# Deformable layer: turning tiles on TensorE by ordinary products with the identity instead of the transpose mode

## The chip, the cores and the metric

The kernel runs on one core of a Trainium2 chip. The metric is the device time of one execution, in microseconds (us). TensorE (PE) multiplies matrices into PSUM, VectorE (DVE) and ScalarE (ACT) work element by element, GpSimd (POOL) issues the indirect DMAs (gathers) here, and SyncE (SP) issues the ordinary DMAs.

## The reference

Four layers are applied one after the other to x of shape (8, 96, 64, 64) in float32: a selective scan over pixels, a layer in the frequency domain, a selective scan in four directions with sampled positions, and a deformable convolution. Each takes the normalised output of the one before. Only the last one is touched by the change. Cut to its core, for each of eight images of 96 channels and 64 x 64 pixels:

```python
om     = conv3x3(x, [offset_w, mask_w]) + [offset_b, mask_b]   # 18 offsets and 9 masks a pixel
mask   = sigmoid(om[18:27])
py, px = pixel position + tap position + offset                # 9 positions a pixel
s[k]   = bilinear(x, py[k], px[k]) * mask[k]                   # 9 sampled vectors of 96 channels
out    = sum over k of weight[:, :, k] @ s[k] + bias
```

The kernel also adds the layer's input to its output.

## The kernel before

Four functions write the four layers one after the other; `layer3` is the deformable one. The pixels of an image stand in 32 tiles of 128, and eight images make 256 tiles. A plan written by hand (`Plan`) gives every piece of work a slot; in each slot the pieces are issued in the fixed order first, pool, main, turn, pe, act, dve, late, sp. Each engine then runs its own pieces strictly in that order and waits on semaphores where data come from another engine. One slot holds one tile, so slot P + i belongs to tile i of the image that starts at slot P.

**What one tile takes.** `gather` (line 1889) has POOL issue nine indirect DMAs, one for each tap, that bring the four neighbours of 128 pixels into the tile `v` (128 x 9 x 4 x 96, a ring of five buffers). `sums` has DVE multiply `v` with the bilinear weights (line 1908) and add the four neighbours (line 1917) into `s` (128 pixels x 9 x 96, a ring of four buffers). `turn` (line 1929) has PE turn the nine 128 x 96 slices of `s` into 96 x 128, three to a PSUM bank `ps_t` (a ring of three). `keep` (line 1938) has ACT copy the three banks into `smp`. After four tiles `out` (line 1961) multiplies `smp` of 512 pixels with the nine weight matrices into `ps_o`, adds the layer's input by a product with the identity (line 1965), ACT adds the bias (line 1970) and SP stores.

**What one image takes ahead of its tiles.** Eight chunks of 512 pixels are loaded and normalised; `turn(c)` (line 1690) turns a chunk in four pieces into `ps_u`, and ACT copies them to `xt`, from which SP writes the table that the gathers read. `offsets(c)` runs the nine taps of the offset convolution (line 1724, `ps_a`), ACT evicts them (line 1736), `back` (line 1741) turns the 27 x 512 result in four pieces, and ACT copies it to `of` (line 1750). Some thirty small DVE and ACT operations make positions and weights of it. This preparation of an image is put into the slots of the image before it.

So three places turn data: line 1690 four times a chunk, line 1741 four times a chunk, and line 1929 nine times a tile: 256, 256 and 2304 turns. Before the change all three call `nc.tensor.transpose(out, x, identity)`. It loads `x` as the stationary operand and streams the identity through it.

Each buffer ring ties two engines: POOL can be five tiles ahead of DVE (`v`), DVE four tiles ahead of PE (`s`), and PE three banks, which is one tile, ahead of ACT (`ps_t`).

Of the kernel before, what the change touches and what calls it, by code (L numbers as in the profile page):

```python
# [170 lines left out]
class Shared:  # L171
# [21 lines left out]
    def stats_tile(self, layer):  # L193

        return new(self.pool, [CH, NB, 2], f"stats{layer}")

    def rsqrt(self, out, var, pool, tag):

        n = var.shape[1]
        ve = new(pool, [CH, n], f"{tag}_ve")  # L200
        self.nc.vector.tensor_scalar(ve, var, EPS, None, ALU.add)
        self.nc.gpsimd.tensor_tensor(  # L202
            out, ve, self.mhalf[:CH, :].to_broadcast([CH, n]), ALU.pow
        )
# [1417 lines left out]
def layer3(S, src, table, dst, st_in, images):  # L1622
# [3 lines left out]
    tc, nc = S.tc, S.nc  # L1626
    NT = NP // 128
    with ExitStack() as ctx:
# [30 lines left out]
        def image(b, P, n):  # L1659
# [5 lines left out]
            start = P - (60, 27, 42, 46, 50)[min(n, 4)]  # L1665
# [20 lines left out]
            def turn(c):  # L1686
                def pe():
                    im["ps"] = ps = new(psu, [128, NW], "ps_u")
                    for j in range(4):
                        nc.tensor.transpose(  # L1690
                            ps[:, j * CH : (j + 1) * CH],
                            im["x", c][:, j * 128 : (j + 1) * 128],
                            S.ident[:CH, :CH],
                        )

                def act():
                    if c == 0:
                        im["xt"] = new(mp, [128, NT, CH], "xt")
                    nc.scalar.copy(
                        im["xt"][:, 4 * c : 4 * c + 4, :].rearrange("p t c -> p (t c)"),  # L1700
                        im["ps"][:, : 4 * CH],
                    )

                plan.at(start + (6 + c if n != 1 else 2 + c), "pe", pe)
                plan.at(start + (7 + c if n != 1 else 3 + c), "first", act)
# [11 lines left out]
            def offsets(c):  # L1717
                def taps(k0, k1):
                    def run():
                        if k0 == 0:  # L1720
                            im["pa"] = new(psa, [128, NW], "ps_a")
                        for k in range(k0, k1):
                            dy, dx = k // 3, k % 3
                            nc.tensor.matmul(  # L1724
                                im["pa"][: 3 * KT, :],
                                om[:, k, :],
                                xpad[:, 8 * c + dy : 8 * c + dy + 8, dx : dx + IW],
                                start=k == 0,
                                stop=k == KT - 1,
                            )  # L1730

                    return run

                def evict():
                    im["oc"] = new(wp, [3 * KT, NW], "oc")
                    nc.scalar.activation(im["oc"], im["pa"][: 3 * KT, :], AF.Identity, bias=omb)  # L1736

                def back():
                    im["ps"] = ps = new(psu, [128, NW], "ps_u")
                    for j in range(4):  # L1740
                        nc.tensor.transpose(  # L1741
                            ps[:, j * 27 : (j + 1) * 27],
                            im["oc"][:, j * 128 : (j + 1) * 128],
                            S.ident[: 3 * KT, : 3 * KT],
                        )

                def keep():
                    if c == 0:
                        im["of"] = new(mp, [128, NT, 3 * KT], "of")
                    nc.scalar.copy(  # L1750
                        im["of"][:, 4 * c : 4 * c + 4, :].rearrange("p t k -> p (t k)"),
                        im["ps"][:, : 4 * 27],
                    )

                t, two = start + 14 + 2 * c, 1
                if n == 0 and c > 1:
                    t, two = P + c - 2, 0
                elif n == 1:
                    t, two = start + 9 + 3 * c // 2, 0
                plan.at(t, "pe", taps(0, 5))  # L1760
                plan.at(t + two, "pe", taps(5, KT))
                plan.at(t + two + 1, "first", evict)
                plan.at(t + two + 1, "pe", back)
                plan.at(t + two + 2, "first", keep)

# [112 lines left out]
        def tiles(im, b, P, n):  # L1878
# [4 lines left out]
            def tile(i):  # L1883
                t, st, g, j = P + i, {}, i // 4, i % 4

                def gather():
                    st["v"] = new(vp, [128, KT, 4, CH], "v")
                    for k in range(KT):
                        nc.gpsimd.indirect_dma_start(  # L1889
                            out=st["v"][:, k].rearrange("p q c -> p (q c)"),  # L1890
                            out_offset=None,
                            in_=flat,
                            in_offset=bass.IndirectOffsetOnAxis(
                                ap=im["idx"][:, i, k : k + 1], axis=0
                            ),
                        )

                def weights():
                    im["ps_w", g] = new(psw, [128, NW], "ps_w")
                    nc.scalar.copy(  # L1900
                        im["ps_w", g][:, : 4 * KT * 4],
                        im["wt"][:, i : i + 4].rearrange("p t k q -> p (t k q)"),
                    )

                def sums():

                    v3 = st["v"].rearrange("p k q c -> p (k q) c")
                    nc.vector.tensor_tensor(  # L1908
                        v3,
                        v3,  # L1910
                        im["ps_w", g][:, j * 4 * KT : (j + 1) * 4 * KT]
                        .unsqueeze(2)
                        .to_broadcast([128, 4 * KT, CH]),
                        ALU.mult,
                    )
                    st["s"] = new(vp, [128, KT, CH], "s", bufs=4)
                    nc.vector.tensor_reduce(  # L1917
                        st["s"],
                        st["v"].rearrange("p k q c -> p k c q"),
                        mybir.AxisListType.X,  # L1920
                        ALU.add,
                    )

                def turn():
                    st["ps"] = []
                    for k0 in range(0, KT, 3):
                        ps = new(pst, [128, NW], "ps_t")
                        for k in range(3):
                            nc.tensor.transpose(  # L1929
                                ps[:CH, k * 128 : (k + 1) * 128], st["s"][:, k0 + k, :], S.ident  # L1930
                            )
                        st["ps"].append(ps)

                def keep():
                    if j == 0:
                        im["smp", g] = new(wp, [CH, KT, NW], "smp")
                    for k0, ps in zip(range(0, KT, 3), st["ps"]):
                        nc.scalar.copy(  # L1938
                            im["smp", g][:, k0 : k0 + 3, j * 128 : (j + 1) * 128],
                            ps[:CH, :384].rearrange("p (k n) -> p k n", k=3),  # L1940
                        )

                plan.at(t - 1, "pool", gather)
                if j == 0:
                    soon = (n, g) in ((0, 0), (0, 2), (1, 0))
                    plan.at(t - (1 if soon else 3), "act", weights)
                plan.at(t, "main", sums)
                plan.at(t + 1, "turn", turn)
                plan.at(t + 2, "first", keep)

# [91 lines left out]
```

## Time and profile before

| | |
|---|---|
| three executions | 18651.31, 18676.62 (median), 18689.72 us |
| the profiled execution | 18651.78 us, its span 18650.0 us |
| deformable layer, about 14900 to 18650 us | 3750 us |
| there: PE busy | 1813.60 us, 5369 matmul and 5368 weight-load records |
| there: DVE busy | 2641.08 us |
| there: POOL busy | 2224.16 us |
| there: ACT busy | 606.34 us |
| granted TensorE clock there (before it) | 0.68 (0.96) |

An engine's rows come from its own instruction records. PE is shown as two tracks: PEld for the weight loads and PE for the matmuls that follow them. A float32 product that isn't in the transpose mode leaves two records on each track for one call in the program. "Idle before" names what ended the idle time ahead of an instruction: an instruction of another engine, "remote" where no recorded instruction fits the semaphore, or "issue" where the engine waited for no semaphore that the profile shows.

### The profile page before, as it was taken

How to read it: one execution, taken by the hardware profiler on the slowest of the kernel's cores; microseconds unless marked ns; L12 is line 12 of the kernel's file. 1: busy time of each engine (PE TensorE's matmuls, PEld its weight loads, DVE VectorE, ACT ScalarE, POOL GpSimd, SP SyncE). 2: the span in 40 equal slices, each digit the busy share in tenths (PEclk: the TensorE clock that was granted, in tenths of full speed). 3: DMA queues.
4: the chain of work that ended last, by engine and by line, in shares of the span. 5: the costliest groups of instructions: out<-in, count | busy, mean ns of one | idle time of the engine just before them, and what ended most of it. 6: DMA issues, size and time to landing. Idle time of an engine off the chain costs nothing. (4 is left out here: it accounts for less than half of the span.)

```text
span 18650.0 us, 134925 instructions
## 1 busy us (share of the span) xinstructions
PE 14905.1 (80%) x35468; PEld 5346.1 (29%) x35468; DVE 16325.1 (88%) x9561; ACT 10781.0 (58%) x17415; POOL 15401.6 (83%) x9600
## 2 busy tenths in 40 slices
PE   8998998848988898989888889888988855454443
PEld 2222223622323232323233233222332212121111
DVE  7999998549999999999999999999999956677777
ACT  7777876536666666666666666666666611111111
POOL 7999997019999999999999999999999955666665
PEclk8999998869999999999999999999999977666666
DMA  7888887349999999999999999999999944444444
GB/s 121 143 147 140 145 144 121 58 106 152 154 154 153 154 154 152 154 153 153 154 152 155 153 153 153 154 151 155 153 153 154 153 131 136 144 146 144 144 145 128
DMA packets 936948, 2689.54 MB, mean 144 GB/s; under 512 B 273906, under 2 KB 275647, under 8 KB 933389
## 3 DMA queue, kind: packets, MB, share of 16 engines
q1 hardware_dynamic: 788717, 2227.78, 70.6%
q0 software_dynamic: 147456, 453.13, 8.2%
q8 instruction: 279, 4.57, 0.1%
q14 instruction: 496, 4.06, 0.1%
HBM read 579.52 MB, written 87.69 MB: 36 GB/s over the span
## 5 line engine op out<-in xcount | busy, mean ns | idle before, releaser
L345 POOL TENSOR_TENSOR dbu<-dd,brep 128x1024 f32<-128x1024 f32 x3840 | 9027.6, 2359 | 459.6 <-DMA dd<-delta 335.8
L362 PE MATMUL ps_y<-dbu,k_red 128*96 128x512 f32 x15360 | 7526.7, 618 | 732.1 <-DVE dbu L354 714.8
L324 ACT ACTIVATE ps_d<-dd,l_alog 128x512 f32<-128x512 f32 x7680 | 5297.8, 690 | 3479.2 <-DVE dbu L354 3305.7
L1449 DVE TENSOR_TENSOR_SCAN ps_d<-ps_d,dbu 128x1024 f32<-128x1024 f32 x2880 | 6589.1, 2288 | 149.4 <-ACT ps_d L324 120.1
L354 DVE TENSOR_TENSOR dbu<-ps_d,crep 128x1024 f32<-128x1024 f32 x3520 | 4312.0, 1225 | 333.9 <-DVE ps_d L1449 7.3
L362 PEld LDWEIGHTS ps_y<-dbu,k_red 128*96 128x96 f32 x15360 | 2358.0, 166 | 5556.3 <-issue 2885.8
L1889 POOL DMA_INDIRECT v<-t,idx x2304 | 2190.2, 951 | 1431.1 <-issue 695.6
L1917 DVE TENSOR_REDUCE s<-v 128x864 f32<-128x3456 f32 x256 | 1559.3, 6091 | 873.7 <-remote 700.2
L1929 PE MATMUL ps_t<-k_ident,s 128*96 128x128 f32 x2304 | 448.9, 343 | 1272.2 <-issue 872.1
L657 DVE TENSOR_TENSOR_SCAN ps_d<-ps_d,carry,dbu 128x1024 f32<-128x1024 f32 x560 | 1315.1, 2348 | 95.1 <-ACT ps_d L673 82.3
L1938 ACT COPY smp<-ps_t 96x384 f32<-96x384 f32 x768 | 332.2, 474 | 1801.0 <-remote 1112.4
L1428 PE MATMUL ps_a<-xs,rep_w 96*128 96x512 f32 x2048 | 1110.1, 623 | 34.1 <-ACT brep L1436 30.2
L1164 PE MATMUL ps_k<-pad,woff 96*96 96x512 f32 x2304 | 1093.4, 597 | 34.1 <-ACT pad L1141 20.8
L1908 DVE TENSOR_TENSOR v<-v,ps_w 128x3456 f32<-128x3456 f32 x256 | 957.7, 3741 | 46.3 <-ACT smp L1938 29.5
L350 POOL TENSOR_TENSOR dbu<-h,crep 128x1024 f32<-128x1024 f32 x320 | 753.6, 2355 | 126.5 <-DVE h L1449 93.1
L1724 PE MATMUL ps_a<-xpad,l_om 96*27 96x512 f32 x1152 | 654.1, 708 | 164.5 <-issue 164.4
L1929 PEld LDWEIGHTS ps_t<-k_ident,s 128*96 128x96 f32 x2304 | 316.9, 156 | 1470.5 <-issue 1083.3
L1961 PE MATMUL ps_o<-smp,l_w 96*96 96x512 f32 x1152 | 555.6, 637 | 31.4 <-issue 31.3
L202 POOL TENSOR_TENSOR sc<-bn_ve,mhalf 96x1 f32<-96x1 f32 (+1 forms) x2 | 1.2, 621 | 695.9 <-DVE mv L972 695.8
L1164 PEld LDWEIGHTS ps_k<-pad,woff 96*96 96x96 f32 x2304 | 372.0, 164 | 674.0 <-issue 587.0
L1428 PEld LDWEIGHTS ps_a<-xs,rep_w 96*128 96x128 f32 x2048 | 346.4, 190 | 750.1 <-ACT brep L1436 311.5
L1386 POOL TENSOR_TENSOR sp_m<-sp_m,sp_s 128x512 f32<-128x512 f32 x384 | 488.2, 1272 | 30.3 <-ACT sp_s L1374 30.3
(259 smaller groups left out, 17100.6 us busy)
## 6 DMA issues: line engine op xcount, KB each, us to landing
dd<-delta SPq DMA_DIRECT2D x3840, 512.0 KB
v<-t,idx POOLq DMA_INDIRECT x2304
xo<-x SPq DMA_DIRECT2D x128, 192.0 KB
x<-xo SPq DMA_DIRECT2D x128, 192.0 KB
x<-x SPq DMA_DIRECT2D x16, 1536.0 KB
yr<-y SPq DMA_DIRECT2D x12, 1536.0 KB
xn<-x SPq DMA_DIRECT2D x64, 192.0 KB
xh<-x SPq DMA_DIRECT2D x16, 768.0 KB
```

The costliest lines, as they stand in the source:

```text
L324: nc.scalar.activation(g.da[:, i, :], g.dd[:, 0, :], AF.Exp, scale=g.a[:, i : i + 1])
L345: nc.gpsimd.tensor_tensor(g.dbu, g.dd[:, 1:2, :].to_broadcast([128, 2, NW]), g.b(), ALU.mult)
L354: nc.vector.tensor_tensor(g.dbu, g.h, g.c(), ALU.mult)
L362: self.S.nc.tensor.matmul(y, self.red[:, 80 - GC * g.n : 176 - GC * g.n], g.dbu[:, i, :], start=first and i == 0, stop=last and i == 1,)
L657: nc.vector.tensor_tensor_scan(out, da, dbu, carry[:, n : n + 1] if c else 0.0, ALU.mult, ALU.add)
L1164: nc.tensor.matmul(ch["pk"][:HD, :], woff[:, k, m * HD : (m + 1) * HD], pad[:, dy : dy + 8, dx : dx + IW], start=k == 0, stop=k == KT - 1,)
L1428: nc.tensor.matmul(dr["pa"], rep_w[:, k, what, s, :], xs[:CH, k % 2, :], start=True, stop=True,)
L1449: nc.vector.tensor_tensor_scan(out[:, way], da[:, way], dbu[:, way], 0.0, ALU.mult, ALU.add)
L1889: nc.gpsimd.indirect_dma_start(out=st["v"][:, k].rearrange("p q c -> p (q c)"), out_offset=None, in_=flat, in_offset=bass.IndirectOffsetOn ...
L1908: nc.vector.tensor_tensor(v3, v3, im["ps_w", g][:, j * 4 * KT : (j + 1) * 4 * KT] .unsqueeze(2) .to_broadcast([128, 4 * KT, CH]), ALU.mult,)
L1917: nc.vector.tensor_reduce(st["s"], st["v"].rearrange("p k q c -> p k c q"), mybir.AxisListType.X, ALU.add,)
L1929: nc.tensor.transpose(ps[:CH, k * 128 : (k + 1) * 128], st["s"][:, k0 + k, :], S.ident)
```

## The change

All three places call a new helper. It issues an ordinary product with the same operands, `x` as the stationary operand and the identity as the moving one, so the result is the same turned tile. Tiles, buffers, order and everything that reads the result stay as they were.

```diff
+    def turn(self, out, x, ident):
+
+        self.nc.tensor.matmul(out, x, ident, start=True, stop=True)
...
-                        nc.tensor.transpose(
+                        S.turn(
                             ps[:, j * CH : (j + 1) * CH],
                             im["x", c][:, j * 128 : (j + 1) * 128],
                             S.ident[:CH, :CH],
...
-                        nc.tensor.transpose(
+                        S.turn(
                             ps[:, j * 27 : (j + 1) * 27],
                             im["oc"][:, j * 128 : (j + 1) * 128],
                             S.ident[: 3 * KT, : 3 * KT],
...
-                            nc.tensor.transpose(
+                            S.turn(
                                 ps[:CH, k * 128 : (k + 1) * 128], st["s"][:, k0 + k, :], S.ident
                             )
```

## The prediction

> **What bounds the kernel now.** The change touches only the last layer, so I first read the busy times by stretch. From 15023 us, the first gather, to 18600 us, just behind the last, POOL's 2304 gathers are busy for 2190.16 of 3577 us, DVE for 2549.15, PE for 1698.43. No engine is full.
>
> Next I read who waited for whom in that stretch. In each row stand the time in total, how often, and the longest.
>
> ```profile
> DVE s L1917 <- remote: 697.7, 45, 48.5
> POOL v L1889 <- DVE s L1917: 543.5, 51, 22.7
> ```
>
> A gather takes 0.95 us plus an issue gap of 0.30, so 1.25; nine make 11.25 us a tile, and 256 tiles 2880 us of the 3577. The remaining 697 are pauses. POOL pauses because its five `v` buffers are full (51 times, 10.7 us each), and they are full because DVE stood still 45 times for 15.5 us ahead of a sum. DVE alone needs 3.74 + 6.09 = 9.83 us a tile, less than POOL.
>
> Why DVE stands still I read in the timeline of one such place (start, duration, engine, line, operation, idle time before it).
>
> ```profile
> 17057.52 1.45 PE L1961 MATMUL ps_o<-smp,l_w 96*96 96x512 f32 x3
> ...
> 17068.64 1.01 PE L1961 MATMUL ps_o<-smp,l_w 96*96 96x512 f32 x1 [1.79 <-issue]
> ...
> 17081.40 0.95 POOL L1889 DMA_INDIRECT v<-t,idx  x1 [0.30 <-issue]
> ...
> 17086.13 5.28 PE L1724 MATMUL ps_a<-xpad,l_om 96*27 96x512 f32 x6 [0.39 <-issue]
> ...
> 17087.60 0.47 ACT L1938 COPY smp<-ps_t 96x384 f32<-96x384 f32 x1 [26.98 <-remote]
> ...
> 17088.33 6.13 DVE L1917 TENSOR_REDUCE s<-v 128x864 f32<-128x3456 f32 x1 [17.66 <-remote]
> ...
> 17094.72 0.94 POOL L1889 DMA_INDIRECT v<-t,idx  x1 [12.38 <-DVE s L1917]
> ```
>
> The reader should see four steps. From 17058 PE issues one record only every 0.7 or 1.4 us, with "issue" before it; ACT and DVE hear nothing from PE. POOL gathers on until its buffers are full at 17082. Some 4 us later PE is quick again, ACT and DVE start within 2 us, and POOL goes on once DVE has freed a `v`. The profile doesn't name what holds PE up.
>
> It does show what the hold-up counts. I took eight uninterrupted runs of gathers, each from the first gather behind a pause to the last before the next, and read the busy times by stretch. Four runs lie where PE has little besides turns, four where it also prepares the next image.
>
> ```profile
> core 0: us, PE busy (x) PEld busy (x) DVE busy (x) ACT busy (x) POOL busy (x), PEclk, DMA share, GB/s
> 16843.20:16921.60 78.40, 25.65 (x82) 10.30 (x80) 60.79 (x13) 6.16 (x15) 59.50 (x63) 0.67 0.68 202
> 17164.70:17243.20 78.50, 30.79 (x90) 14.81 (x88) 67.35 (x27) 14.98 (x31) 59.61 (x63) 0.65 0.56 167
> 18209.40:18299.10 89.70, 28.63 (x84) 12.84 (x82) 71.45 (x15) 6.37 (x15) 68.04 (x72) 0.63 0.54 159
> 18424.70:18514.30 89.60, 27.31 (x84) 12.84 (x82) 71.36 (x15) 6.26 (x14) 67.98 (x72) 0.63 0.54 159
> 16982.30:17027.00 44.70, 32.55 (x85) 9.84 (x83) 32.66 (x7) 4.39 (x11) 34.01 (x36) 0.77 0.52 153
> 17037.60:17082.30 44.70, 29.77 (x77) 9.40 (x75) 32.76 (x7) 3.68 (x9) 34.01 (x36) 0.73 0.52 154
> 17426.20:17470.90 44.70, 30.21 (x82) 9.48 (x81) 32.72 (x7) 4.13 (x10) 34.01 (x36) 0.77 0.52 153
> 17873.00:17929.00 56.00, 29.04 (x90) 10.45 (x88) 41.05 (x9) 4.75 (x12) 42.55 (x45) 0.74 0.52 154
> ```
>
> The runs last from 44.7 to 89.7 us and hold 36 to 72 gathers, four to eight tiles. But PE's records, matmuls and loads together, number 152 to 178 in each. A run of gathers ends when PE has issued about 165 records, however long that took. Time, gathers and ACT's records (9 to 31) vary too much to be what is counted. So the number of PE records sets how often the layer pauses: 10,134 records in the stretch over 51 pauses are 199 a pause.
>
> [...]
>
> **The change part by part.** Only PE's stream changes; waits, signals, buffers, DMAs and the order stay.
>
> ```profile
> L1961 PE MATMUL ps_o<-smp,l_w 96*96 96x512 f32 x1152 | 555.6, 637 | 31.4 <-issue 31.3
> L1929 PE MATMUL ps_t<-k_ident,s 128*96 128x128 f32 x2304 | 448.9, 343 | 1272.2 <-issue 872.1 <-ACT smp L1938 354.6 <-DVE s L1917 31.6
> ```
>
> *Records.* Line 1961 is called 576 times (64 groups by nine) and has 1152 matmul records, two a call; line 1929 is called 2304 times and has 2304, one a call. So a turn grows from one load and one matmul to two of each: 2 x 2816 = 5632 more records, of which I count 5500 in the stretch (the first image's preparation precedes the gathers). 10,134 become 15,630.
>
> *PE's time.* In the timeline at 17042 us and full clock the turns follow each other every 0.109 us. The nearest ordinary products, 96 columns moving (line 867), come 40 in 3.20 us, 0.080 each, so 128 columns take 0.107, twice for one call: 0.21 in place of 0.11. That is 0.98 us a tile and some 300 us in all, or 600 at half clock. PE has 1879 idle us in the stretch; it is hidden there. If it weren't, 0.98 us of a tile's turn would stand in the chain of a pause.
>
> [...]
>
> *Pauses.* At 199 records a pause, 15,630 make 78.5, 27.5 more. At 10.7 us each that is +294. But a pause lets PE run freely, and after it there are twice the turn records ready; I give each pause 20 more records (half of one tile's 36), so 219: 71.4 pauses, 20.4 more, +218. I take the middle, +256, and a third of the 0.98 us for 75 pauses, +25, since a pause's chain holds one tile's turns at most and often none. Sum: 18651.8 + 281 = 18933 for the profiled execution. The runs' median lies 25 us above it, so 18958; I say 18950.
>
> *Bounds.* Upwards: 27.5 pauses at what DVE loses, 15.5, plus 0.98 for 78.5 pauses: +503. Downwards: 40 more records a pause give 65 pauses, and with the shortest of the regular pauses, behind a run of three tiles, 8.6 us, 14 x 8.6 = +120. So the forecast's own range is 18770 to 19155. Below nothing it can't go without the third rival.
>
> **Rivals.** *Hidden.* The hold-up counts something that goes along with PE's records but isn't doubled: tiles, signals, or calls. Then only PE's hidden 300 us are added and the time is 18650 to 18700. For it: the cause isn't named. Against it: the eight runs differ twofold in tiles and threefold in ACT's records.
>
> *Worse.* While the next image is prepared, a tile's share of PE is 28 records plus 26 of preparation now, and 46 + 34 = 80 then. The four tiles that wait in `s` behind a pause need 320, more than a run allows, so PE never catches up and DVE stands at every tile. It decides if a run there falls under three tiles and pauses grow over 15 us: 78.5 at 15.5 are 1217, less today's 697, +520 or more: 19170 to 19350.
>
> *Faster.* The ordinary product might raise the granted clock, 0.68 in this stretch. Behind the pause above, six taps take 5.28 us (0.85 each), where at full clock they are 0.43 apart. If turns at full clock signal DVE 1 to 2 us earlier in each of 51 pauses, and the number of pauses stays, that is -50 to -100: 18550 to 18600. It decides if the clock there rises over 0.9 with still some 51 pauses. Against it: in the row above PE's first work behind a pause is taps, not turns, and DVE started at 17088.33 without waiting for them.
>
> **How the numbers follow.** Forecast 0.70, worse 0.10, hidden 0.12, faster 0.08. The likeliest gives 18950. The range leaves out the faster case and somewhat over half of the hidden one below, and half of the worse one above, 0.20 together: 18680 to 19260. No change is within 0.2% (37 us), the spread of the three runs: faster 0.08, same 0.12, slower 0.80.
>
> **What would show it.** Right: line 1929 with 4608 matmul records; runs of gathers still with about 150 to 190 PE records but fewer tiles, four to five in the light stretches and about three in the preparation; 65 to 80 waits of POOL for line 1917 with 9 to 12 us each; layers before 14900 us unchanged. Wrong: runs with the same tiles and 230 or more records (then records aren't counted), pauses of the same number but longer (then PE's time counts), or no second record a turn.

## The result, and the profile after

The changed kernel takes 18875.11 us (median of four executions, 18858.41 to 18877.99), the kernel before 18678.14 (18651.31 to 18689.72). The ratio is 1.0106, with a 95% interval of 1.0088 to 1.0123: slower by 197 us. The profiled execution has a span of 18872.2 us, 222 more than before.

All of it lies in the last layer; up to 14900 us the busy times of both kernels agree within 0.1%. There the first rows to read are the costliest groups (busy time and mean duration, then the idle time before them).

```profile
L199 PE MATMUL ps_t<-k_ident,s 128*96 128x128 f32 x4608 | 756.8, 324 | 1355.7 <-issue 889.0
...
L199 PEld LDWEIGHTS ps_t<-k_ident,s 128*96 128x96 f32 x4608 | 659.7, 198 | 1523.0 <-issue 1057.2
```

The turns of the tiles now have 4608 records on each track in place of 2304, two a call. What one tile's turns cost PE stands in the timeline: nine turns at full clock (granted 1.00 in both places), first of the kernel before, then of the changed one (start, duration, number of records).

```profile
17042.09 1.19 PE L1929 MATMUL ps_t<-k_ident,s 128*96 128x128 f32 x9
```

```profile
17175.74 2.21 PE L199 MATMUL ps_t<-k_ident,s 128*96 128x128 f32 x18
```

The records still follow each other every 0.109 us, but there are 18: 1.02 us more a tile. Next come the waits in the stretch of the gathers (total, how often, longest).

```profile
POOL v L1893 <- DVE s L1921: 750.0, 78, 17.6
DVE s L1921 <- remote: 683.1, 53, 32.7
DVE s L1921 <- PE ps_t L199: 200.7, 22, 21.8
```

DVE's standing still ahead of its sum is spread over two rows here. Before, the second of them was this:

```profile
DVE s L1917 <- PE ps_t L1929: 108.1, 11, 18.4
```

So DVE stood still 75 times for 884 us, in place of 56 times for 806 us.

POOL now pauses 78 times for DVE, 27 times more, and 750 us, 206.5 us more. That is nearly the whole difference: the rest of the 222 are 13 us by which the first gather starts later (15036.5 in place of 15023.5 us; in the later runs, of whichever kernel, it starts anywhere from 15014 to 15059, so I read nothing into it) and a few us at the end. In the same stretch PE has 7799 + 7798 records, 200 for each of the 78 pauses. Before they were 199.

Last the runs of gathers, picked as before: the first two while the next image is prepared, the third across two stretches, the last two where nothing is prepared.

```profile
core 0: us, PE busy (x) PEld busy (x) DVE busy (x) ACT busy (x) POOL busy (x), PEclk, DMA share, GB/s
17068.10:17101.60 33.50, 25.59 (x85) 9.97 (x83) 23.04 (x5) 3.48 (x8) 25.53 (x27) 0.86 0.51 151
17186.10:17219.90 33.80, 25.95 (x87) 10.26 (x85) 23.10 (x5) 3.48 (x8) 25.52 (x27) 0.88 0.51 150
17754.30:17821.80 67.50, 18.92 (x82) 12.05 (x80) 58.86 (x29) 8.95 (x18) 51.33 (x54) 0.65 0.56 168
18465.40:18510.10 44.70, 14.54 (x61) 8.67 (x59) 32.62 (x7) 2.56 (x5) 34.02 (x36) 0.68 0.55 162
18579.80:18624.40 44.60, 14.32 (x65) 8.93 (x63) 32.54 (x7) 2.96 (x6) 33.94 (x36) 0.66 0.54 161
```

In the preparation a run holds 27 gathers, three tiles, where it held four; in the light stretch 36, four tiles, where it held seven or eight. The records of PE in a run are 162 to 172 in the first three, but only 120 and 128 in the last two.

These five runs were picked, as the prediction's eight were. Counted from the traces' gathers alone, there are 57 gaps of more than 1.5 us before and 80 after. All the runs behind a gap of 6 us or more number 49 before and 66 after. The middle one (median) holds 156 records and 36 gathers before, 142.5 and 27 after. 42 of the 49 and 57 of the 66 lie between 100 and 200 records; the others reach from 0 to 263 and from 46 to 285.

### The profile page after: what moved, and what is told of

It is laid out like the page before. It is cut to its first block, busy times and chain, and to the rows that moved or that the text cites. A ratio compares the mean times of both kernels' runs of the same rounds, so it can differ in the third digit from the quotient of the medians.

```text
span 18872.2 us, 140557 instructions
## 1 busy us (share of the span) xinstructions
PE 15298.5 (81%) x38284; PEld 5782.9 (31%) x38284; DVE 16330.3 (87%) x9561; ACT 10807.1 (57%) x17415; POOL 15401.7 (82%) x9600
## 5 line engine op out<-in xcount | busy, mean ns | idle before, releaser
L199 PE MATMUL ps_t<-k_ident,s 128*96 128x128 f32 x4608 | 756.8, 324 | 1355.7 <-issue 889.0
L199 PEld LDWEIGHTS ps_t<-k_ident,s 128*96 128x96 f32 x4608 | 659.7, 198 | 1523.0 <-issue 1057.2
L1965 PE MATMUL ps_o<-smp,l_w 96*96 96x512 f32 x1152 | 605.4, 666 | 134.7 <-issue 134.1
L1728 PE MATMUL ps_a<-xpad,l_om 96*27 96x512 f32 x1152 | 586.1, 659 | 20.9 <-issue 20.8
```

The source lines that it names most:

```text
L199: self.nc.tensor.matmul(out, x, ident, start=True, stop=True)
```

## The experiments

Each group of experiments ran on one chip, with the kernel before beside it. Two of the four chips behaved unlike the one of the result, and that became the main finding, so the groups are told in order.

**First group: the parts, on a chip without the hold-up.** The kernel before takes 17961.86 us here (median of 31 executions, 17941.78 to 17996.66), 716 less than in the result.

e1_tile_turns: only line 1929 becomes an ordinary product.

```diff
-                            nc.tensor.transpose(
-                                ps[:CH, k * 128 : (k + 1) * 128], st["s"][:, k0 + k, :], S.ident
+                            nc.tensor.matmul(
+                                ps[:CH, k * 128 : (k + 1) * 128], st["s"][:, k0 + k, :], S.ident,
+                                start=True, stop=True,
                             )
```

> Only the nine turns of a tile (line 1929) become ordinary products; the turns of the preparation stay in the transpose mode. Theory A (the number of PE records sets how often the gathers must pause): 4608 of the 5632 added records, so 0.82 of the 197 us that the whole change cost, +161, about 18840. Rival P (the preparation's turns are what costs, since their bank has one buffer only): +40 at most, about 18700.

e2_turns_twice: every turn twice in the transpose mode, at all three places.

```diff
-                        for k in range(3):
+                        for k in (0, 0, 1, 1, 2, 2):
...
-                    for j in range(4):
+                    for j in (0, 0, 1, 1, 2, 2, 3, 3):
```

> The kernel before, with every turn issued twice in the transpose mode, the second over the first. Records and PE time of the turns are those of the changed kernel, the mode is that of before. Theory A: +197, about 18875, runs of gathers of three to four tiles. Rival M (the ordinary mode itself holds PE up, through its clock or its switch of mode): no change, 18650 to 18700.

e3_tiny_products: a product of one column ahead of each of a tile's turns.

```diff
+                            nc.tensor.matmul(
+                                ps[:1, k * 128 : k * 128 + 1], st["s"][:, k0 + k, :1],
+                                S.ident[:, :1], start=True, stop=True,
+                            )
                             nc.tensor.transpose(
```

> The kernel before, with a tiny ordinary product (one column by one column) ahead of each of a tile's nine turns, whose output the turn overwrites: 9216 more PE records, little PE time. Theory A: 9216 / 5632 x 197 = +322, about 19000. Rival T (PE's time behind a pause is what costs): at 0.03 to 0.06 us for each of 18 matmuls a tile 0.5 to 1.1 us, so 0.5 to 1.1 of the change's cost, +100 to +220, about 18780 to 18900.

e5_half_columns: the changed kernel, with the residual first and the nine products over 256 columns.

```diff
-                            st["po"][:CH, :], w[:, k, :], im["smp", g][:, k, :],
-                            start=k == 0, stop=False,
+                            st["po"][:CH, : NW // 2], w[:, k, :], im["smp", g][:, k, : NW // 2],
+                            start=False, stop=k == KT - 1,
```

> The changed kernel, with the nine products of line 1961 over half of the 512 columns (the other half of the result holds the residual and bias alone, so a part of the convolution is left out). The records are those of the changed kernel; PE's time falls by 18 x 0.21 us a group, 0.96 us a tile, which is what the change had added. Theory A: as the changed kernel, 18840 to 18890. Rival T: back to the kernel before, about 18680.

| kernel | PE records added | median, us | ratio, interval |
|---|---|---|---|
| e1_tile_turns | 4608 | 17965.68 | 1.0001, 0.9991 to 1.0011 |
| e2_turns_twice | 5632 | 17960.38 | 1.0003, 0.9993 to 1.0012 |
| e3_tiny_products | 9216 | 17966.42 | 1.0001, 0.9992 to 1.0011 |
| e5_half_columns | 5632 | 17971.76 | 1.0002, 0.9993 to 1.0012 |

Every theory that gave a cost missed. Why, the waits and the busy times of e2_turns_twice tell.

```profile
POOL v L1889 <- issue: 693.0, 2275, 0.3
...
POOL v L1889 <- DVE s L1917: 0.3, 1, 0.3
```

```profile
15026.00:17918.00 2892.00, 1921.75 (x7883) 1103.76 (x7881) 2583.28 (x754) 587.33 (x1272) 2186.26 (x2303) 0.80 0.59 176
```

POOL pauses for DVE once, for 0.3 us. All its gathers take 2892 us, close to the 2880 of 256 x 11.25, and PE's 15,764 records pass in that time without holding POOL up. On this chip POOL is the bound of the layer and PE's extra work is hidden, whatever its mode. The layer's 697 us of pauses, and with them the cost of the change, belong to a condition that isn't always there. The changed kernel itself was not run on such a chip; e1 with 4608 of its 5632 added records and e5 with all of them come nearest.

The trace's records show one more difference. In the four profiles of this chip 36,857 to 36,864 landing signals of the gathers are recorded, sixteen for each of the 2304; in the profile of the kernel before that the prediction read, 5835 are, and 7292 in that of the changed kernel. In the layers before, both kinds of profile have about the same number of landing records, some 68,600 to 68,900.

**Second group: the changed kernel once more, and a pause made on purpose.** On this chip the hold-up is back: the kernel before takes 18673.12 us.

> The changed kernel itself, beside the kernel before. In the runs of the result the kernel before took 18678 us and POOL paused 51 times for DVE; in the first four experiments it took 17962 and POOL gathered without a pause, and no change of PE's records moved the time. Theory C (the hold-up of PE is a condition of the chip or of the recording in that measurement, and the change costs time only under it): if the kernel before takes about 17960 here, the changed one takes the same, 17940 to 17990; if it takes about 18680, the changed one takes about 18875. Rival A (PE's records cost time whatever the condition): +1% in both.

Measured: 18845.61 us, 1.0096, 1.0079 to 1.0112. With e1 to e5 this is theory C: the cost is there where the hold-up is, and not where it isn't. Rival A falls.

e7_pool_breaks: every third tile, POOL first copies 96 columns of the last gather, so it waits for the landing.

```diff
+                    if i % 3 == 0 and "last" in im:
+                        nc.gpsimd.tensor_copy(S.rest, im["last"][:, KT - 1, 3, :])
+                    im["last"] = st["v"]
                     for k in range(KT):
```

> The kernel before, with a small copy on POOL ahead of every third tile's gathers that waits for the landing of the tile before: 80 breaks, each the landing time of 2.9 us plus an operation of about 1 us. Theory C: without the hold-up POOL is the bound of the layer, and the breaks add 80 x 3 to 4 us = 240 to 320, about 18240; under the hold-up they let PE run free before its 165 records are used up, and 80 x 4 us take the place of 51 x 10.7 to 13.6, so 100 to 370 us less, 18310 to 18580. Rival (a short break doesn't let PE run free): under the hold-up +240 to +320.

Measured: 18595.14 us, 0.9963, 0.9950 to 0.9975, so 78 less where at least 100 less was expected. The waits:

```profile
POOL v L1893 <- DVE s L1921: 320.9, 36, 12.6
...
POOL rest L1890 <- DMA v<-t,idx: 182.4, 77, 5.8
```

36 pauses for DVE are left of 51, and they cost 223 us less; the breaks' own waiting, 182.4 us, and their copies, 80 of 0.26 us (where about 1 us each was expected), take nearly all of that back. Most of the 78 us lies elsewhere: POOL's other waits for DVE behind the first gather are 84.7 us in place of 143.6, and why they are shorter isn't shown. A break frees PE at some places only. Of two runs of gathers, both with a break ahead of them, the first also has a long pause for DVE there.

```profile
16884.20:16917.70 33.50, 27.72 (x83) 9.29 (x81) 23.02 (x5) 4.40 (x11) 25.57 (x27) 0.91 0.51 151
16837.50:16871.10 33.60, 0.00 (x0) 0.00 (x0) 13.72 (x4) 0.00 (x0) 25.62 (x27) 0.50 0.50 151
```

The first, behind a break and then 10.6 us for DVE, begins with PE free and holds 164 records. Ahead of the second POOL had rested for about 2.6 us, and PE issues nothing at all in it. The trace has 60 runs behind a rest of 2.5 to 3.5 us; in 17 of them PE issues at least 28 records for each tile gathered, in the others fewer, in four none. So a long pause of POOL frees PE, as the prediction read it, and a rest of about 3 us mostly doesn't.

**Third group: records against time, under the hold-up.** The kernel before takes 18662.08 us. Three kernels of the first group ran again, and one with fewer records:

> The kernel before with every turn issued twice in the transpose mode, once more, for a chip on which the kernel before takes about 18670. Theory A (under the hold-up PE's records set how often POOL pauses): as the changed kernel, +170 to +200, about 18855. Rival M (the ordinary mode itself holds PE up): no change. Where the kernel before takes about 17960 it tells nothing new: the same as before.

> The kernel before with nine tiny ordinary products a tile, once more; 9216 more PE records, little PE time. Under the hold-up theory A: 9216 / 5632 x 172 to 197 = +280 to +320, about 18970. Rival T (PE's time behind a pause): +100 to +220 at most. Without the hold-up: the same as before.

> The changed kernel with line 1961's products over half of the columns, once more (that half of the convolution is left out); records of the changed kernel, PE time of the one before. Under the hold-up theory A: 18820 to 18880, as the changed kernel. Rival T: about 18670. Without the hold-up: the same as before.

e11_fewer_taps:

```diff
-                        for k in range(k0, k1):
+                        for k in (range(2) if k0 == 0 else range(8, 9)):
...
-                    for k in range(KT):
+                    for k in range(3):
                         nc.tensor.matmul(
                             st["po"][:CH, :], w[:, k, :], im["smp", g][:, k, :],
```

> The kernel before with three taps in place of nine in the offset convolution and in the products of line 1961 (six taps of both sums are left out): 3072 PE records fewer. Under the hold-up theory A: 3072 / 5632 x 172 to 197 = 94 to 107 less, or 3072 / 199 x 10.7 = 165 less, so 18510 to 18580. Without the hold-up: POOL stays the bound, 17900 to 17970.

| kernel | PE records, against before | median, us | against before, us | ratio, interval | us per 1000 records |
|---|---|---|---|---|---|
| e11_fewer_taps | -3072 | 18558.20 | -104 | 0.9948, 0.9931 to 0.9965 | 34 |
| e8_turns_twice_again | +5632 | 18823.42 | +161 | 1.0084, 1.0068 to 1.0101 | 29 |
| e10_half_columns_again | +5632 | 18836.70 | +175 | 1.0090, 1.0073 to 1.0107 | 31 |
| e9_tiny_again | +9216 | 18924.46 | +262 | 1.0136, 1.0120 to 1.0153 | 28 |

The change itself gave +197 and +172 for 5632 records, 35 and 31 us per 1000. Rival M falls: in the transpose mode twice as many turns cost about as much as ordinary ones. The size is under what was expected in e8 and e9 and within it in e10; the intervals are too wide to say that the price of a record falls with their number.

Rival T needs more care, since the two edits that were to part records from time do so only in part. The tiny products are not quick: at full clock nine of them with their turns take 3.34 us in e3 (17021.26 to 17024.60 us), where nine ordinary turns take 2.21 and nine in the transpose mode 1.19. The 2.15 us beyond the turns are 0.12 for each of the 18 tiny matmul records, where 0.03 to 0.06 was expected. And e10 shortens the products, not the turns themselves. What PE was busy for from 14900 us to the end stands in the next rows, in the order of the table. Before the change it was 1813.60 us, in the changed kernel 2197.20.

```profile
14900.00:19000.00 4100.00, 1186.11 (x3883) 568.06 (x3882) 2667.82 (x844) 637.14 (x1390) 2258.89 (x2339) 0.64 0.45 129
14900.00:19000.00 4100.00, 2130.21 (x8212) 1075.14 (x8212) 2664.14 (x833) 637.83 (x1376) 2246.28 (x2333) 0.73 0.45 129
14900.00:19000.00 4100.00, 1987.89 (x8209) 1206.76 (x8207) 2652.16 (x829) 636.18 (x1373) 2237.36 (x2330) 0.70 0.45 128
14900.00:19000.00 4100.00, 2580.28 (x10024) 1006.60 (x10024) 2673.22 (x842) 648.24 (x1389) 2253.18 (x2338) 0.67 0.45 129
```

Against before that is -627, +317, +174 and +767 us of PE's time, and +384 for the change. If time were what is paid for, a us of it would cost 0.17, 0.51, 1.00 and 0.34 us, a sixfold spread; per 1000 records the five kernels pay 28 to 35. So the records carry the cost, and PE's time alone can't. A small share of time beside them isn't ruled out, and as every edit adds or removes a load together with a matmul, it stays open which of the two is counted. Rival P, that the preparation's turns cost, can't be all of it either: e9 leaves them alone and costs the most.

The row of POOL's waits, for e11_fewer_taps, then for e9_tiny_again:

```profile
POOL v L1889 <- DVE s L1917: 461.8, 45, 16.9
```

```profile
POOL v L1889 <- DVE s L1917: 774.3, 83, 18.1
```

The pauses go from 45 over 51 (before), 74 to 78 (5632 more records) to 83, and each takes 9 to 11 us. From the first gather to the end PE has 7308, 10,317, 15,869 and 19,533 records, so 162, 202, 203 to 214 and 235 a pause. In the runs behind a gap of 6 us or more alone, the median is 138.5, 156, 142.5 to 160 and 161 records, while that of the gathers falls from 49.5 over 36 to 27 and 27.

**Fourth group: what else might count.** This chip has no hold-up: 17958.91 us for the kernel before.

e12_act_records:

```diff
+                    for _ in range(18):
+                        nc.scalar.copy(S.tiny, S.one)
                     for k0, ps in zip(range(0, KT, 3), st["ps"]):
```

> The kernel before with 18 tiny copies on ACT ahead of each tile's three (4608 ACT instructions more, none on PE; about 0.2 us each, 4 us a tile of an ACT that is busy for 545 of 3577 us). Under the hold-up: if it counts PE's records alone, the time rises by 0 to 60 us (a pause's chain holds some of the copies), about 18690; if all engines' records count alike, 4608 at the 0.03 us that each PE record cost is +140, about 18810. Without the hold-up: the same as before, to +20.

Measured: 17963.34 us, 1.0006, 0.9996 to 1.0016. It says only that 4608 more records of ACT are hidden here; whether ACT's records count under the hold-up stays open.

e13_breaks_two: as e7_pool_breaks with `i % 2` in place of `i % 3`.

> The kernel before with POOL's break ahead of every second tile instead of every third: 120 breaks of 2.9 us are 348 us. A tile has 28 PE records, 54 while the next image is prepared, so two tiles stay under 110. Under the hold-up: if a break lets PE run free, few of the 51 pauses are left, 2880 + 348 + about 110 at the start of the layer in place of 3577, about 18430; if a break often fails to do so, as it did in some places with every third tile, 18550 to 18650. Without the hold-up POOL is the bound and it costs some 330, about 18290.

Measured: 18302.63 us, 1.0190, 1.0173 to 1.0207, so +344 where some 330 were expected. The breaks wait for their landing 120 times:

```profile
POOL rest L1890 <- DMA v<-t,idx: 293.8, 120, 6.0
```

With the small copies themselves (0.26 us, 120 times) that is 325 us, nearly the whole loss: without the hold-up the time that the breaks took from POOL was time of the kernel. So e7's breaks beat the kernel before under the hold-up alone, by 0.4%, and this kind of break is no gain elsewhere.

## Why the prediction was right, step by step

**What bounds the layer: right, for the chip that was measured.** POOL's gathers with the pauses between them set the time there. That the pauses aren't a property of the kernel could not be seen in one profile; on two chips they are missing, and POOL alone is the bound. The forecast holds because the result came from a chip with the hold-up; by e1 to e5 it would have missed on the others.

**What the hold-up counts: right.** Over e8 to e11 and the change the cost for 1000 records stays at 28 to 35 us, while the cost for PE's time varies sixfold. "About 165" a run was too firm a number, read from eight picked runs with 152 to 178: 42 of all 49 lie between 100 and 200, and in the changed kernel's last stretch two end at 120 and 128. In records for each pause of the whole stretch, 199 before and 200 after, it held better than I had trusted it to.

**The records of the change: right.** Two a call, 4608 matmul records in line 199's tile turns; 15,597 in the stretch where 15,630 were counted.

**PE's time: right, and hidden.** 0.98 us a tile was worked out, 1.02 measured. On a chip without the hold-up e1 and e2 put all of it under POOL's gathers at no cost; under the hold-up e10 took 209 of the added 384 us of PE's busy time out again, and with +175 us the cost stayed.

**The price of the pauses: the term that was mis-sized.** I had taken the middle of 20.4 and 27.5 more pauses at 10.7 us each, +256, and +25 for the turns in their chain. There were 27 more, the upper of my two counts, but a pause costs 750.0 / 78 = 9.6 us now, and the sum is +206.5. The count was taken too low and the price too high, so two errors partly cancel in the forecast. The extra records I gave each pause weren't there. The +25 for the turns in a pause's chain is not seen in pauses that got shorter, but no run takes it out by itself: e10 keeps the turns at twice their time.

**The rivals.** Hidden holds where there is no hold-up, with ratios of 1.0001 to 1.0003 for e1 to e5. I gave it 0.12 by asking what the hold-up counts; the better question was whether it is there at all. Worse did not come: 17 of the 66 runs counted above are shorter than three tiles, where 5 of 49 were, but the pauses didn't grow. Faster neither: the granted clock in the stretch is 0.71 in place of 0.68. The "six taps" in that case were misread: the row has six records, so three taps; the spacing is that of the records and stands.

**The supply of instructions.** Whether PE waits for its instructions to be brought can be read in the traces, under the hold-up too. The packets of one DMA queue of the kind "instruction" grow with PE's records, first in the kernel before, then in the changed one:

```profile
q8 instruction: 279, 4.57, 0.1%
```

```profile
q8 instruction: 301, 4.93, 0.1%
```

22 more for 5632 records are 256 a packet; e1 has 297, 18 more for 4608, and e3 315, 36 more for 9216, so 256 again. The other queue of that kind has 496 in all of them. If PE waited for such a packet, one would come between POOL's stop and PE's recovery. That is so in none of the 49 pauses of 6 us or more before the change and in one of the 66 after. So PE recovers without new instructions being brought, which speaks against their supply as the cause.

**What stays open** is the cause. The hold-up and the missing landing records go together in every profile here: six with the hold-up among the experiments (5315 to 8380 of the gathers' 36,864 landings recorded) besides the two of the result, and all of them without most of the landings. Every time in this study is that of a recorded execution, so it isn't shown whether a hold-up of the recording holds PE up, or one thing slows both, nor whether the hold-up is there in an execution that isn't recorded.

## What to carry to other kernels

Look at how often a stage stops, and what is the same in each stretch between two stops; where it is a count of one engine's instructions, as the 199 and 200 PE records a pause are here, an edit that is hidden in that engine's busy time can still cost (+172 and +197 us for the change). Before a tuning step rests on stalls whose releaser the profile can't name, run the unchanged kernel on another chip: here it was 4% faster there, and added PE records that cost 1% under the hold-up cost nothing. Turning by ordinary float32 products cost PE here 18 records on each track for a tile's nine turns in place of 9 and, at full clock, 2.21 us in place of 1.19, and it gained nothing in any run.

## What the hardware showed that was not expected

The same program takes 17935 to 17997 us on two chips and 18646 to 18711 in the other three measurements (the result's and those of the second and third group). While POOL gathers without a pause in the latter, PE issues one record every 0.7 or 1.4 us, at times 2.1 (so from 17060 to 17086 us of the kernel before), mostly after 100 to 200 records, or none at all (the 33.6 us run of e7), until POOL has stopped for some time, about 4 us in the place that the prediction shows. On one of the former two, e2 runs its 2304 gathers with a single wait for DVE's sums, of 0.3 us.
